# Moving a never-taken branch of a fused RWKV and mixture-of-experts kernel ahead of the last expert's products

## The chip, the cores and the metric

The kernel runs on one core of a Trainium2 chip. The metric is the device time of one execution in microseconds (us). Three runs of the kernel before took 984.41, 988.21 and 988.93 us; the median is 988.21 us. One execution was also profiled, instruction by instruction.

TensorE is written PE here (its weight loads PEld), VectorE DVE, ScalarE ACT, GpSimd POOL and SyncE SP. A "q" behind a name (PEldq, POOLq) marks what the engine's sequencer does by itself: branches, semaphore waits, drains. L1002 is line 1002 of the kernel's file.

## The reference, cut to what matters

```python
x = x + rwkv(layernorm(x), ...)        # time mixing: 4 sequences of 1024 tokens, 256 channels
x = x + moe(layernorm(x), ...)         # 8 experts, 2 for each token

def moe(hidden):                       # 256 -> 896 -> 256
    weights = softmax(hidden @ gate_w.T)
    # each token goes to its two best experts; in one sequence an expert
    # takes at most capacity = 320 tokens, in order of the tokens
    h1, h3 = dispatch @ w1, dispatch @ w3
    return combine(silu(h1) * h3 @ w2)
```

With four sequences an expert gets between 0 and 1280 rows; the mean is 4096 x 2 / 8 = 1024. How many it gets is known only at run time.

## The kernel before

**Layout of the work.** The time mixing goes block by block (256 tokens) through the four sequences. After each group of tokens the router writes the rows, by scatters on POOL, into a buffer in device memory (`disp`). There each expert owns 11 tiles of 128 rows. The tiles are worked on in five stages, `TILES = (0, 1, 3, 5, 9, 11)` (L42): stage 0 is tile 0 of every expert, stage 3 is tiles 5 to 8, and stage 4 is tiles 9 and 10, the rarely filled ones. The constant `B` is 4 and `E` is 8, so stage 4 is written `B` in the code.

**One expert's stage** is the generator `expert(e, s)` (L839). It issues four loads on SP: the weights w1, w3, w2 (`load_w`, L834, memory tag "w", five buffers) and the rows `xe` (L852). PE transposes the rows (L873), DVE copies them to `xeT` (L877). Then `hidden` (L887) makes seven pairs of products with w1 and w3 (L904), ACT takes silu (`sl`, L909), DVE multiplies (`act`, L893, eight buffers, of which one stage of an expert holds seven at a time). `results` (L919) multiplies by w2 (L925), DVE scales by the router's weight (`ye`, L929), and POOL adds each tile of 128 rows to the output by an indirect DMA (L932). Each such DMA carries explicit dependencies on the previous expert's output DMAs (`last["adds"]`), since two experts add to the same token's row.

**The order.** `experts_in_turn` (L979) takes a list of (expert, stage) jobs. For each job it yields the seven pairs of products, then starts the next job's loads and transposes ("ahead"), then finishes the results. Stages 0 to 2 are interleaved with the time mixing; stage 3 of the eight experts runs after it, one expert after the other, and PE has nothing else to do there. In stage 3 only three of the four tiles are sure to be needed (`SURE = 3`). The fourth stands inside `tc.If(flags(e) > 0)` (L1002). In this data the branch is taken for three experts and skipped for five, expert 6 and expert 7 among these. Stage 4 of all eight experts stands in one last branch, `tc.If(flags(E) > 0)` (L1150), at the very end. It is never taken in this data.

**What a branch is.** On each of the five engines it is a compare-and-branch, the taken body, and a short body for "not taken". The short body waits until the engine itself has done all that it had been given, then raises the engine's semaphores by as much as the taken body would have. On POOL it also waits for the outstanding indirect DMAs and raises their semaphores with one instruction (INC_SWDGE_SEM); on SP it waits for outstanding loads where the body holds loads. No engine waits for another there. The compiler's scheduler places instructions around a branch per engine; it may put instructions that come earlier in the program behind a branch, and later ones in front of it. In the trace of before, DVE's last `ye` and POOL's last output DMA of an expert come behind that expert's branch.

After the last branch each engine drains, SP waits for every DMA and engine semaphore, and two barriers over all engines end the program (line L1188 in the profile).

Of the kernel before, what the change touches and what calls it, by code (L numbers as in the profile page):

```python
# [9 lines left out]
F32 = mybir.dt.float32  # L10
# [7 lines left out]
P = 128  # L18
B, T, C = 4, 1024, 256
NT = B * T  # L20
H, N = 16, 16
CC = C // P
HC = H // CC
TB = 256
# [3 lines left out]
RT = RB // P  # L28
RPS = T // RB
ST = T // P  # L30
E, FF = 8, 896
FC = FF // P
# [13 lines left out]
W = C + 1 + E  # L46
# [19 lines left out]
def rwkv_then_moe_kernel(  # L66
# [12 lines left out]
    nc = tc.nc  # L79

    const = ctx.enter_context(tc.tile_pool(name="const", bufs=1))
    keep = ctx.enter_context(tc.tile_pool(name="keep", bufs=1))
    a1 = ctx.enter_context(tc.tile_pool(name="a1", bufs=1))
    a2 = ctx.enter_context(tc.tile_pool(name="a2", bufs=2))
    sm = ctx.enter_context(tc.tile_pool(name="sm", bufs=1))
    fp = ctx.enter_context(tc.tile_pool(name="ffn", bufs=2))
# [4 lines left out]
    def bank(tag, name):  # L91
        return ps.tile(
            [P, 512], F32, tag=tag, name=name, bufs={"m": 4, "y": 1, "f": 3}[tag])
# [42 lines left out]
    def maa(m, cc):  # L136
# [10 lines left out]
        out=tri, in_=ones, pattern=[[1, P]], compare_op=ALU.is_ge, fill=0.0,  # L147
# [5 lines left out]
        out=bd, in_=ones[:, :HC], pattern=[[-N, HC]], compare_op=ALU.is_ge, fill=0.0,  # L153
# [3 lines left out]
        out=bd, in_=bd, pattern=[[N, HC]], compare_op=ALU.is_ge, fill=0.0,  # L157
# [36 lines left out]
    wmat = const.tile([P, H, P], F32, tag="wmat", name="wmat")  # L194
# [639 lines left out]
    def load_w(ap, rows_, nm):  # L834
        t = fp.tile([P, rows_, FF * CC // rows_], F32, tag="w", name=nm, bufs=5)
        nc.sync.dma_start(out=t, in_=ap.rearrange("(k p) n -> p k n", p=P))
        return t

    def expert(e, s):  # L839

        nm = f"{e}_{s}"
        n = TILES[s + 1] - TILES[s]
        r0 = e * SLOTS + TILES[s] * P
        after = tc.issue_after(cleared) if s == 0 and e < 2 else nullcontext()
        with after:
            w1e = load_w(w1[e], CC, f"w1_{nm}")
            w3e = load_w(w3[e], CC, f"w3_{nm}")
            w2e = load_w(w2[e], FC, f"w2_{nm}")  # L850
        xe = fp.tile([P, n, W], F32, tag="xe", name=f"xe{nm}")
        load = nc.sync.dma_start(  # L852
            out=xe, in_=disp[r0:r0 + n * P, :].rearrange("(s p) c -> p s c", p=P)).ins
        for g in range(len(SEGMENTS)):
# [8 lines left out]
                    reason="rows of this expert")  # L863
        if s < B:
            tc.add_to_no_dep_group(f"load{s}", load)
        xeT = fp.tile([P, CC, n * P], F32, tag="xeT", name=f"xeT{nm}")
        pts = [bank("f", f"pe{nm}")] * CC
        if n > 2:
            pts[1] = bank("f", f"pe{nm}_1")
        for cc in range(CC):  # L870
# [11 lines left out]

        def tag(t0):

            return "m" if t0 else "f"

        def hidden(t0, t1):  # L887
            lo, w = t0 * P, (t1 - t0) * P
            acts = []

            def product(sl, p3, f):
                act = fp.tile([P, w], F32, tag="act", name=f"act{nm}_{t0}_{f}", bufs=8)
                nc.vector.tensor_tensor(act, sl, p3[:, :w], ALU.mult)  # L893
                acts.append(act)

            for f in range(FC):
                p1 = bank(tag(t0), f"p1_{nm}_{t0}_{f}")
                if 2 * w <= 512:
                    p3 = p1[:, w:]
                else:  # L900
                    p3 = bank(tag(t0), f"p3_{nm}_{t0}_{f}")
                for pp, wt in ((p1, w1e), (p3, w3e)):
                    for cc in range(CC):
                        nc.tensor.matmul(  # L904
                            pp[:, :w], wt[:, cc, f * P:(f + 1) * P], xeT[:, cc, lo:lo + w],
                            start=cc == 0, stop=cc == CC - 1,
                        )
                sl = fp.tile([P, w], F32, tag="sl", name=f"sl{nm}_{t0}_{f}")
                nc.scalar.activation(sl, p1[:, :w], AF.Silu)  # L909
                if f:  # L910
                    product(*held)
                held = sl, p3, f
                yield 2 * CC * w
            product(*held)
            return acts
# [3 lines left out]
        def results(t0, t1, acts):  # L919
            ye = fp.tile([P, t1 - t0, C], F32, tag="ye", name=f"ye{nm}_{t0}", bufs=3)  # L920
            for t in range(t0, t1):
                i = t - t0
                po = bank(tag(t0), f"pw2_{nm}_{t}")
                for f in range(FC):
                    nc.tensor.matmul(  # L925
# [43 lines left out]
    def due(s):  # L969
        g = AFTER[s]  # L970
        return g in clock.routed and clock.step >= clock.routed[g] + LAGS[s]

    def flags(e):

        if "flags" not in last:
            _, last["flags"] = nc.values_load_multi_w_load_instructions(last["over"][0:1, :])
        return last["flags"][e]

    def experts_in_turn(jobs):  # L979

        ahead = None
        for i, (e, s) in enumerate(jobs):
            while ahead is None:
                if s >= B or due(s):
                    ahead = expert(e, s)
                    clock.turn = min(s, B - 1)
                    yield next(ahead)
                    yield None
                else:
                    yield None  # L990
            now, ahead = ahead, None
            for _ in range(FC):
                yield next(now)
            if i + 1 < len(jobs) and (jobs[i + 1][1] >= B or due(jobs[i + 1][1])):
                ahead = expert(*jobs[i + 1])
                clock.turn = jobs[i + 1][1]
                yield next(ahead)
            for cols in now:
                if cols is not None:
                    yield cols  # L1000
                    continue
                with tc.If(flags(e) > 0):  # L1002
                    for _ in now:
                        pass

    def routed(b, r):
# [12 lines left out]
    def fronts(n):  # L1019
        if n >= NBLK:  # L1020
            return iter(()), None
        b, blk = divmod(n, BPS)
        o = Block()
        return front(b, blk, o), o

    work = experts_in_turn([(e, b) for b in range(B) for e in range(E)])


# [7 lines left out]
    f, cur = fronts(0)  # L1036
# [27 lines left out]
    with tc.issue_after(cleared):  # L1064
        r0 = (B - 1) * T
        nc.sync.dma_start(
            out=out[r0:r0 + EK * P, :].rearrange("(k p) c -> p k c", p=P),
            in_=empty[0][:, :, :C])
# [13 lines left out]
    with tc.manual_schedule(engines={ENG.PE}):  # L1082
        for n in range(NBLK):
# [11 lines left out]
            c = [chunk(b, blk, t, cur) for t in range(TPB)]  # L1095
            new = back(b, blk, cur)
            for i, stage in enumerate((
# [23 lines left out]
                while credit > 0 or drain:  # L1121
                    drain = False
                    cols = next(work, None)
# [23 lines left out]
        nc.vector.tensor_copy(last["over"], over)  # L1147
        for _ in work:
            clock.step += 1
    with tc.If(flags(E) > 0):  # L1150
        for _ in experts_in_turn([(e, B) for e in range(E)]):
            pass


# [37 lines left out]
```

## Time and profile before

| | us |
|---|---|
| median of three runs | 988.21 |
| the profiled execution | 987.89 |
| its span, first to last instruction | 986.2 |
| PE busy | 943.5 (96%) |
| expert 6, stage 3: products with w1, w3 on PE | 920.26 to 938.48 |
| expert 6: results on PE | 939.20 to 948.53 |
| expert 7, stage 3: products with w1, w3 on PE | 948.83 to 967.13 |
| expert 7: results on PE, the last matmul's end | 966.96 to 976.19 |
| last output DMA on POOL | 976.99 to 978.54 |
| end of the span | 986.17 |

Times inside the profile count from the first instruction. The difference of 1.7 us between the profiled execution's time and its span lies outside what the profile shows. The page gives an engine's busy time, groups of instructions by line with the idle time ahead of them and what ended it, and the granted clock of TensorE (PEclk, 1.00 is full speed). Sequencer rows are not busy time; they are read from the view of a single line.

### The profile page before, as it was taken

What the parts mean: (1) busy time and instruction counts of PE and PEld (TensorE: products, weight loads), DVE (VectorE), ACT (ScalarE), POOL (GpSimd) and SP (SyncE); (2) the same over time, 40 slices, a digit from 0 to 9 for tenths busy, and PEclk for the clock granted to TensorE, in tenths of its full rate; (3) what the DMA queues carried; (4) which work ended last, traced back from release to release, by engine and by line L of the source; (5) the groups of instructions that cost most, each with busy time, mean ns of one, the idle gap of its engine ahead of it and who ended that gap; (6) DMA issues with size and microseconds to landing.
All of it is one profiled execution on the core that took longest, in us unless ns stands there. A gap on an engine that the chain in (4) does not pass through costs nothing. (4 is left out here: it accounts for less than half of the span.)

```text
span 986.2 us, 17107 instructions
## 1 busy us (share of the span) xinstructions
PE 943.5 (96%) x6758; PEld 748.7 (76%) x6758; DVE 454.5 (46%) x1317; ACT 318.2 (32%) x797; POOL 249.1 (25%) x267
## 2 busy tenths in 40 slices
PE   7899889999999799999999999999999999999995
PEld 6667677888788588887888788888866866867764
DVE  7888857666676544435453434422222222222221
ACT  6636545544653532243414123211110111111110
POOL 6321512422117312111163211361111111211111
PEclk9999999999999999999999999999999999999998
DMA  4995132534435544342465544586545235433421
GB/s 154 264 288 187 50 99 98 199 119 132 156 122 206 162 124 126 104 145 73 122 183 173 157 134 156 158 272 182 156 144 151 44 113 150 134 81 103 145 54 19
DMA packets 92073, 139.06 MB, mean 141 GB/s; under 512 B 5456, under 2 KB 73552, under 8 KB 91984
## 3 DMA queue, kind: packets, MB, share of 16 engines
q1 hardware_dynamic: 79120, 120.36, 37.6%
q0 software_dynamic: 12720, 17.47, 9.2%
q8 instruction: 58, 0.95, 0.4%
q14 instruction: 31, 0.25, 0.1%
q10 hardware_dynamic: 144, 0.02, 0.0%
HBM read 103.45 MB, written 34.39 MB: 140 GB/s over the span
## 5 line engine op out<-in xcount | busy, mean ns | idle before, releaser
L904 PE MATMUL p<-xeT,w 128*128 128x256 f32 (+2 forms) x1960 | 430.6, 374 | 3.6 <-DVE act L893 1.8
L904 PEld LDWEIGHTS p<-xeT,w 128*128 128x128 f32 x1960 | 326.3, 191 | 93.8 <-issue 8.6
L893 DVE TENSOR_TENSOR act<-sl,p 128x256 f32<-128x256 f32 (+2 forms) x245 | 99.2, 407 | 294.3 <-ACT sl L909 178.2
L909 ACT ACTIVATE sl<-p 128x256 f32<-128x256 f32 (+2 forms) x245 | 91.0, 374 | 438.8 <-PE p L904 436.2
L925 PE MATMUL pw<-w,act 128*128 128x256 f32 x938 | 210.5, 380 | 1.2 <-DVE act L893 1.2
L932 POOL DMA_INDIRECT y_out<-ye,xe x67 | 105.4, 1573 | 405.0 <-DVE ye L929 346.9
L925 PEld LDWEIGHTS pw<-w,act 128*128 128x128 f32 x938 | 175.3, 190 | 25.7 <-DVE act L893 2.3
L929 DVE TENSOR_SCALAR ye<-pw,xe 128x256 f32<-128x256 f32 x67 | 32.2, 483 | 126.0 <-PE pw L925 125.9
L499 DVE TENSOR_TENSOR aw<-pa,wmat 128x512 f32<-128x512 f32 x128 | 79.3, 682 | 8.0 <-PE pa L491 8.0
L416 PE MATMUL pc<-xm,wa 128*128 128x256 f32 x256 | 68.6, 417 | 10.1 <-DVE xm L406 5.9
L804 POOL DMA_INDIRECT disp<-hs,is x64 | 63.9, 998 | 26.8 <-issue 15.5
L416 PEld LDWEIGHTS pc<-xm,wa 128*128 128x128 f32 x256 | 51.2, 207 | 22.2 <-DVE xm L406 6.2
L340 ACT ACTIVATE aside<-x 128x256 f32<-128x256 f32 x60 | 24.9, 416 | 82.2 <-DVE x L604 81.4
L406 DVE SCALAR_TENSOR_TENSOR xm<-xx,ch,xT 128x256 f32<-128x256 f32 x96 | 42.8, 477 | 12.5 <-POOL xx L400 7.7
L491 PE MATMUL pa<-rT,kT 32*128 32x256 f32 x512 | 40.2, 401 | 0.7 <-DVE upd L539 0.7
L520 PE MATMUL y<-aw,vpad 128*32 128x128 f32 x1024 | 40.5, 278 | 0.0
L443 POOL TENSOR_TENSOR xm_g<-xx,ch 128x512 f32<-128x512 f32 x16 | 17.7, 1109 | 84.6 <-PE pc L416 75.4
L550 POOL TENSOR_TENSOR state<-state,upd 128x64 f32<-128x64 f32 x24 | 8.2, 341 | 120.4 <-DVE upd L539 109.2
L599 PE MATMUL po<-wa,zT 128*128 128x256 f32 x128 | 30.8, 383 | 6.1 <-DVE zT L591 4.5
L520 PEld LDWEIGHTS y<-aw,vpad 128*32 128x32 f32 x1024 | 24.4, 109 | 12.2 <-issue 11.4
L491 PEld LDWEIGHTS pa<-rT,kT 32*128 32x128 f32 x512 | 25.2, 184 | 8.5 <-issue 3.5
L453 PE MATMUL pt<-wa,xm 128*128 128x256 f32 x128 | 30.8, 383 | 0.9 <-DVE rbT L436 0.9
(183 smaller groups left out, 826.1 us busy)
## 6 DMA issues: line engine op xcount, KB each, us to landing
w<-w_in SPq DMA_DIRECT2D x96, 896.0 KB, 6.0
disp<-empty SPq DMA_DIRECT2D x8, 795.0 KB, 14.3
disp<-empty SPq DMA_DIRECT2D x16, 265.0 KB, 7.2
xe<-disp SPq DMA_DIRECT2D x16, 265.0 KB, 2.7
xe<-disp SPq DMA_DIRECT2D x8, 530.0 KB, 3.7
y_out<-x SPq DMA_DIRECT2D x8, 512.0 KB, 3.0
x<-x_in SPq DMA_DIRECT2D x7, 512.0 KB, 6.5
wa<-w_attn_in SPq DMA_DIRECT2D x5, 256.0 KB, 4.3
```

Source lines behind the costliest of these rows:

```text
L406: last["xm"] = nc.vector.scalar_tensor_tensor(xm[:, cc, :], xx[:, cc, :], maa(m, cc), xT[:, cc, 1:TB + 1], ALU.mult, ALU.add,).ins
L416: nc.tensor.matmul(pp[:, m * TB:(m + 1) * TB], wa[w][:, cc, m * P:(m + 1) * P], xm[:, cc, :], start=cc == 0, stop=cc == CC - 1,)
L491: nc.tensor.matmul(pa[g][:, cc * TB:(cc + 1) * TB], o.kT[rows32, cc, cols], o.rT[rows32, cc, :, cols], start=True, stop=True, tile_positio ...
L499: nc.vector.tensor_tensor(w.rearrange("p q i -> p (q i)"), pa[g], wmat[:, 4 * g:4 * g + 4, :].rearrange("p q i -> p (q i)"), ALU.mult,)
L520: nc.tensor.matmul(y[32 * g:32 * g + 32, :], o.vp[:, t, cc * 4 + g, q * 32:(q + 1) * 32], aw[g][:, cc * 2 + q, :], start=state is None and ...
L804: ins = nc.gpsimd.indirect_dma_start(out=disp[:, :], out_offset=bass.IndirectOffsetOnAxis(ap=idx_s[g][:, c, t:t + 1], axis=0), in_=last["h ...
L893: nc.vector.tensor_tensor(act, sl, p3[:, :w], ALU.mult)
L904: nc.tensor.matmul(pp[:, :w], wt[:, cc, f * P:(f + 1) * P], xeT[:, cc, lo:lo + w], start=cc == 0, stop=cc == CC - 1,)
L909: nc.scalar.activation(sl, p1[:, :w], AF.Silu)
L925: nc.tensor.matmul(po[:, :C], acts[f][:, i * P:(i + 1) * P], w2e[:, f, :], start=f == 0, stop=f == FC - 1,)
L929: nc.vector.tensor_scalar_mul(ye[:, i, :], po[:, :C], xe[:, t, C + 1 + e:C + 2 + e])
L932: ins = nc.gpsimd.indirect_dma_start(out=out[:, :], out_offset=bass.IndirectOffsetOnAxis(ap=xe.bitcast(I32)[:, t, C:C + 1], axis=0), in_=y ...
```

## The change

The branch with stage 4 leaves the end of the program and moves into `experts_in_turn`, behind the flag branch of the last expert but one (expert 6, stage 3). At that place expert 7's stage 3 has been started ("ahead": its loads are issued or queued, its rows transposed), and its products with w1, w3, w2 follow behind the moved branch. The program now ends with the flag branch of expert 7.

So that the branch does not take the memory in which expert 7's operands stand, its tiles lie elsewhere: w1 and w3 in halves in the buffers of `x` (tag "x", four buffers, each half loaded by a DMA of its own), w2 in the buffer of `wmat`, the rows in tag "hs", the transposed rows in tag "xx", and the PSUM banks under tag "m" in place of "f". The time mixing and the router have left these; the last access to any of them in the trace of before is at 656.9 us. The tags `act`, `sl` and `ye` are still shared. No buffer changes its size. For stages 0 to 3 the code is as before.

```diff
+    class Halves:
+        def __init__(self, ap, nm):
+            self.parts = []
+            for cc in range(CC):
+                t = keep.tile([P, RT, C], F32, tag="x", name=f"w{nm}_{cc}", bufs=4)
+                t = t.rearrange("p t c -> p (t c)")[:, :FF]
+                nc.sync.dma_start(out=t, in_=ap[cc * P:(cc + 1) * P, :])
+                self.parts.append(t)
...
     def expert(e, s):
...
+        if s < B:
...
+        else:
+            w1e, w3e = (Halves(ap[e], f"{i}_{nm}") for i, ap in ((1, w1), (3, w3)))
+            w2e = const.tile([P, H, P], F32, tag="wmat", name=f"w2_{nm}").rearrange(
+                "p h i -> p (h i)")[:, :FC * C].rearrange("p (f c) -> p f c", f=FC)
+            nc.sync.dma_start(out=w2e, in_=w2[e].rearrange("(k p) n -> p k n", p=P))
+            xe = a2.tile([P, RT, W], F32, tag="hs", name=f"xe{nm}")[:, :n, :]
...
-        pts = [bank("f", f"pe{nm}")] * CC
+        pts = [bank("f" if s < B else "m", f"pe{nm}")] * CC
...
-            return "m" if t0 else "f"
+            return "m" if t0 or s >= B else "f"
...
                 with tc.If(flags(e) > 0):
                     for _ in now:
                         pass
+            if jobs[i + 1:] == [(E - 1, B - 1)]:
+                with tc.If(flags(E) > 0):
+                    for _ in experts_in_turn([(k, B) for k in range(E)]):
+                        pass
...
         for _ in work:
             clock.step += 1
-    with tc.If(flags(E) > 0):
-        for _ in experts_in_turn([(e, B) for e in range(E)]):
-            pass
```

More of the change, by code (lines that the diff above doesn't have):

```diff
@@ L837, in load_w, with __getitem__ @@
         return t
+    class Halves:
[6 more added lines that the diff above has]
+                self.parts.append(t)
+        def __getitem__(self, at):
+            rows_, cc, cols = at
+            return self.parts[cc][rows_, cols]
     def expert(e, s):
@@ L846, in expert @@
         after = tc.issue_after(cleared) if s == 0 and e < 2 else nullcontext()
[L847 to L851, printed above, removed]
+        if s < B:
+            with after:
+                w1e = load_w(w1[e], CC, f"w1_{nm}")
+                w3e = load_w(w3[e], CC, f"w3_{nm}")
+                w2e = load_w(w2[e], FC, f"w2_{nm}")
+            xe = fp.tile([P, n, W], F32, tag="xe", name=f"xe{nm}")
+        else:
[4 more added lines that the diff above has]
+            xe = a2.tile([P, RT, W], F32, tag="hs", name=f"xe{nm}")[:, :n, :]
         load = nc.sync.dma_start(
@@ L865, in expert @@
             tc.add_to_no_dep_group(f"load{s}", load)
-        xeT = fp.tile([P, CC, n * P], F32, tag="xeT", name=f"xeT{nm}")
-        pts = [bank("f", f"pe{nm}")] * CC
+        if s < B:
+            xeT = fp.tile([P, CC, n * P], F32, tag="xeT", name=f"xeT{nm}")
+        else:
+            xeT = a1.tile([P, CC, TB], F32, tag="xx", name=f"xeT{nm}")
+        pts = [bank("f" if s < B else "m", f"pe{nm}")] * CC
         if n > 2:
```

## The prediction

> **What bounds the kernel now.** I read the page's busy shares first, then the timeline around expert 6 and the end, then the lines of the two branches one by one, then the granted clock in windows.
>
> ```profile
> PE 943.5 (96%) x6758; PEld 748.7 (76%) x6758; DVE 454.5 (46%) x1317; ACT 318.2 (32%) x797; POOL 249.1 (25%) x267
> ```
>
> PE is busy for 96% of the span. What matters is whether PE idles, and what lies behind its last matmul. The timeline:
>
> ```profile
> 939.20 9.33 PE L925 MATMUL pw<-w,act 128*128 128x256 f32 x42
> 948.83 18.30 PE L904 MATMUL p<-xeT,w 128*128 128x384 f32 x56 [0.30 <-PEq L1002]
> ...
> 966.96 9.23 PE L925 MATMUL pw<-w,act 128*128 128x256 f32 x42
> 976.99 1.55 POOL L932 DMA_INDIRECT y_out<-ye,xe  x1 [1.47 <-DVEq L1150]
> ```
>
> The second row is expert 7's first products: a skipped flag branch (L1002) costs PE 0.30 us. The last matmul ends at 976.19, the span at 986.17: 9.98 us of tail. The view of line L1150, the branch that moves:
>
> ```profile
> L1150 PEldq COMPARE_BRANCH  x1: 3650/3650/3650, 976.4 to 976.4; - x1
> L1150 POOLq COMPARE_BRANCH  x1: 45/45/45, 976.8 to 976.8; - x1
> L1150 DVEq EVENT_SEMAPHORE  x1: 21/21/21, 976.8 to 976.8; - x1
> L1150 PEldq EVENT_SEMAPHORE  x1: 51/51/51, 980.1 to 980.1; - x1
> L1150 POOLq INC_SWDGE_SEM  x1: 1012/1012/1012, 980.8 to 980.8; - x1
> ```
>
> and PE's row for the eight flag branches (three of them taken, which gives 11 records), with the end (L1188):
>
> ```profile
> L1002 PEldq COMPARE_BRANCH  x11: 70/180/356, 747.5 to 972.2; - x11
> ```
>
> ```profile
> L1188 POOLq DRAIN  x3: 46/107/3458, 981.9 to 985.9; - x3
> ```
>
> (Columns: count, shortest/median/longest in ns, first and last start in us.) On PE the moved branch takes 3.65 us, a flag branch at most 0.36. It jumps over eight experts: 28 + 14 products of two passes and 4 transposes, each pass a weight load and a matmul, are 176 instructions for an expert, 1408 in all; a flag branch jumps over 140. The instruction queue moved 0.95 MB in 58 packets, and one packet of 16 KB started at 977.69, inside the 3.65 us: PE was waiting for its code. Now this costs nothing: PE has no work left, and POOL's last output DMA lands only at about 980.75, when its wait for it ends.
>
> **The change, part by part.**
>
> *What PE pays.* Behind the end of expert 6's results PE's queue would hold: flag branch, moved branch, expert 7's products. At the end of before, semaphore to semaphore of the two branches is 976.24 to 980.09, so 3.85 us, all of it PE idle if nothing stands between them. Something may: the moved branch must come behind expert 6's last output DMA (its first output DMA depends on that one), and that DMA is issued at 949.33, when PE has already started on expert 7. Matmuls of expert 7 that the scheduler puts ahead of the branch run while the code is fetched. The trace shows the rates: at 944.50 PE's sequencer reached the flag branch, with 4.03 us of matmuls (18 pairs) still to run, so it runs ahead; the 84 instructions of those results were handed out from 939.2 to 944.5, 0.063 us each, 0.13 for a pair, while a pair with 384 columns runs for 18.30 / 56 = 0.327. Each pair ahead thus hides about 0.2 us. The bounds: no pair ahead, 3.85; and 16 pairs, 3.85 - 16 x 0.2 = 0.65. More is not possible by much, since expert 7 may hold one of the eight `act` buffers at most when the branch needs seven. I take the four pairs that run between 948.83 and the issue of expert 6's last output DMA (0.5 us, rounded up to whole products of one pair of operands): 3.85 - 4 x 0.2 = **+3.0**.
>
> *What the clock takes.* PE then idles for about 3.0 to 3.3 us. The windows view (us; PE, PEld, DVE, ACT, POOL busy; PEclk; DMA) shows what followed such a gap:
>
> ```profile
> 120.70:124.10 3.40, 1.24 (x11) 0.80 (x12) 2.92 (x15) 3.32 (x12) 0.73 (x3) 1.00 0.47 155
> 124.10:127.50 3.40, 3.40 (x9) 2.58 (x10) 1.62 (x3) 2.34 (x7) 0.00 (x0) 0.50 0.57 149
> ...
> 328.90:332.30 3.40, 0.28 (x2) 0.28 (x3) 2.10 (x4) 1.58 (x5) 2.22 (x3) 1.00 0.54 161
> 332.30:335.70 3.40, 3.40 (x12) 2.77 (x11) 3.37 (x12) 0.00 (x0) 1.71 (x2) 0.50 0.74 227
> ```
>
> At 328.9 PE had idled 3.19 us for a load; in the next 3.4 us the clock was 0.50 and eight matmuls took 607 ns each against 379 elsewhere. A window with 1.24 us of work was followed by half a clock too. Half a clock for 3.4 us of work loses 1.7. The windows' edges are fixed (the two drops are 61 x 3.41 us apart), so it depends on where the gap falls: it must put over some 2.1 us into one window. A gap of 3.0 does so in (0.41 + 2 x 0.9) / 3.41, two of three cases. I take 1.0 (bounds 0 and 1.7).
>
> [...]
>
> *What the tail gives back.* Without the branch, POOL needs no wait for the last landing and no INC_SWDGE_SEM (1.01) ahead of its drain. It can drain from 978.54, the end of its last output DMA's instruction, in place of 981.88. With its 3.46 us it is through at 982.0 in place of 985.34 (times as in before, PE's delay left out): **-3.34**. Next late is then SP: its waits go on from the landing at 980.75 and, by their present pace (twelve waits and the drain from 981.80 to 983.1, so 1.2 us for what follows this landing), end at about 982.0 too, so a shorter drain would give no more. At worst the drain can only start to count from the landing: 980.75 + 3.46 = 984.2, a gain of 1.1. I take 3.3, since the drain has no semaphore to wait for.
>
> *What costs nothing, and its cover.* ACT's and DVE's part of the branch is 45 + 17 and 56 + 21 ns; DVE's next instruction for expert 7 came at 951.75, three us behind its last `ye`. SP: w2 of expert 7 was issued at 948.65; behind the moved branch's eight waits (0.5 us; every earlier load has landed) it would be issued some 1 us later, lands within 6.6 and is needed at 966.96. POOL: the branch waits for expert 6's last output DMA (until about 954.4) and takes 1.0; POOL's next work came at 970.95. Should one of these jumps wait for code as PE's did, 3.65 us fit into each of these covers but DVE's, and DVE's work is itself delayed by PE's gap. The new tiles: their loads and copies lie in the branch that isn't taken; the extra DMAs (six for an expert in place of four) are not issued. Stages 0 to 3 keep their buffers, and what `x`, `hs`, `xx` and `wmat` held was last used at 656.9 us.
>
> **Sum:** +3.0 + 1.0 - 3.3 = +0.7 us. From the profiled execution's 987.89 that is **988.6**; the three runs' median, 988.21, lies 0.3 above the profiled execution, which is far inside their own spread of 4.5 us.
>
> **How it could go otherwise.**
>
> *The fetch is hidden.* The scheduler waits for expert 6's last output DMA to land (3.8 to 5.1 us behind its issue) before it places the branch, so that 12 to 16 pairs run first. PE then pays about 0.7 and no clock is lost: 0.7 - 3.3 = -2.6, so **985.3**, and 984.8 if PE pays as little as 0.2. For it: the dependency is on the data, not on the issue. Against: the output DMAs of one expert's branch may be ordered by issue alone.
>
> *The tail is not given back.* The drain starts to count at the landing (gain 1.1), and PE pays in full, with the clock: 3.85 + 1.4 - 1.1 = +4.2, so **992.1**. For it: that drain is 3.46 us long, and the profile names nothing that it waits for.
>
> *Slower: a second fetch.* PE's jump lands near the end of a block of code. At the end of before the next block's packet started only at 980.79, 3.1 us behind the first one's and 0.7 behind the end of the branch; like the first (977.69, usable at 980.03) it would be usable 2.3 later, 3.0 us behind PE's restart. So if fewer than 9 pairs plus what the queue takes ahead, some 20 to 30 of a block's 235 instructions (0.95 MB for PE's 13,516 are 70 bytes each), are left where the jump lands, PE stops again, by up to 3 us, and the clock stays at one half for two windows, 3.4 lost in place of 1.0: 0.7 + 3.0 + 2.4 = +6.1, so **994.0**. That place is decided by the code's length alone: about 1 in 9.
>
> *It doesn't do what it says.* The scheduler could put the branch behind expert 7's products after all; the `act` buffers exclude it, since all seven would be held.
>
> **How the numbers follow.** A measurement of this kernel can tell about 0.5% from no change, 4.9 us. The forecast (986.8 to 990.5 by its own bounds) has 0.50; the hidden fetch 0.22; the tail not given back 0.14; the second fetch 0.11; no effect 0.03. The range takes in all but the second fetch: from 984.8 (hidden fetch at its best) to 992.4 (full price, full loss of clock, 1.1 from the tail: +4.45). Faster by over 0.5% means below 983.0, which only the hidden fetch with a still shorter tail reaches: 0.06. Slower means above 992.8: the second fetch and a third of the tail's case, 0.16. Within: 0.78.
>
> **What would show it.** PE's row of the moved branch again near 3.65 us, at about 949 to 953; a gap in PE's timeline of 3.0 to 4.2 us there, by its length the number of matmuls ahead; PEclk 0.50 in the window behind it; no INC_SWDGE_SEM behind POOL's last output DMA, and a tail of 6.6 us in place of 9.98. It is wrong if PE's branch is short in its new place (then the time falls by 3 us), if the tail keeps its 9.98, or if the gap exceeds 5 us.

## The result, and the profile after

The changed kernel's median is 990.73 us over 11 runs, against 987.5 us for the kernel before in its 11. One run of the kernel before, at 4534 us, was disturbed; without it the median of the other ten is 986.9, and the ratio leaves it out. The ratio is 1.0034, with a 95% interval of 1.002 to 1.0048: about 3.3 us slower, clear of noise, though inside 0.5%. The profiled execution is the slowest of the 11 (993.48 us, span 991.7), so the terms read from its trace may be larger than the usual ones.

The view of the moved branch's line, after (columns: count, shortest/median/longest in ns, first and last start in us):

```profile
L1032 POOLq EVENT_SEMAPHORE  x4: 17/43/6601, 950.1 to 956.9; - x4
L1032 DVEq COMPARE_BRANCH  x1: 56/56/56, 949.1 to 949.1; - x1
L1032 PEldq COMPARE_BRANCH  x1: 5085/5085/5085, 949.3 to 949.3; - x1
L1032 PEldq EVENT_SEMAPHORE  x1: 51/51/51, 954.4 to 954.4; - x1
L1032 POOLq INC_SWDGE_SEM  x1: 935/935/935, 957.0 to 957.0; - x1
```

DVE passes in 56 ns. POOL waits 6.6 us for the output DMAs and holds up nobody, since its next work is at 979.65. PE waits 5.09 us for its code, in place of 3.65. PE's timeline (start, length, count; in brackets the idle time ahead and what ended it):

```profile
939.73 9.33 PE L951 MATMUL pw<-w,act 128*128 128x256 f32 x42
954.65 21.18 PE L930 MATMUL p<-xeT,w 128*128 128x384 f32 x56 [5.59 <-PEq L1032]
975.67 9.23 PE L951 MATMUL pw<-w,act 128*128 128x256 f32 x42
```

The second row starts 5.59 us behind the end of the first, where it was 0.30, and lasts 21.18 us, where it was 18.30. The windows view says why (us; busy us of PE, PEld, DVE, ACT, POOL; PEclk; DMA share; GB/s):

```profile
949.00:952.50 3.50, 0.06 (x1) 0.00 (x0) 0.48 (x1) 0.00 (x0) 1.55 (x1) 1.00 0.76 147
952.50:956.00 3.50, 1.35 (x2) 0.84 (x3) 0.00 (x0) 0.00 (x0) 0.00 (x0) 0.66 0.73 203
956.00:959.50 3.50, 3.50 (x7) 1.92 (x6) 0.00 (x0) 0.49 (x1) 0.00 (x0) 0.50 0.01 1
959.50:963.00 3.50, 3.50 (x10) 1.96 (x10) 0.55 (x1) 0.49 (x1) 0.00 (x0) 0.86 0.00 0
963.00:966.50 3.50, 3.50 (x12) 2.08 (x11) 1.11 (x2) 0.49 (x1) 0.00 (x0) 1.00 0.02 5
```

The granted clock fell to one half, for 6.83 us in all (953.6 to 960.5 in the trace's clock records): 7 matmuls in a window that holds 12 at full clock. The first two rows also show the DMA engines 76% and 73% busy. Part of that is expert 7's w2, issued at 949.18, 0.07 us ahead of PE's branch:

```profile
949.18 0.37 SPq L836 DMA_DIRECT2D w<-w_in  x1
```

The tail:

```profile
L1214 POOLq DRAIN  x3: 46/113/5359, 985.5 to 991.4; - x3
L1214 SPq DRAIN  x3: 7/7/7, 990.0 to 991.1; - x3
```

From the last matmul's end (984.90) to the end of the span (991.66) it is 6.76 us, where it was 9.98.

The sum for this execution: the gap +5.29 (5.59 - 0.30), the half clock +2.88 (21.18 - 18.30), the tail -3.22: +4.95. The spans differ by 5.5; the other 0.5 was there before the change begins to act (the end of expert 6's results is at 949.06, in place of 948.53). Over all runs the difference is 3.3.

### The profile page after: what moved, and what is told of

It reads as the page before. It is cut to its first block, busy times and chain, and to the rows that moved or that the text cites. A ratio compares the mean times of both kernels' runs of the same rounds, so it can differ in the third digit from the quotient of the medians.

```text
span 991.7 us, 17110 instructions
## 1 busy us (share of the span) xinstructions
PE 946.3 (95%) x6758; PEld 750.0 (76%) x6758; DVE 454.7 (46%) x1317; ACT 318.5 (32%) x797; POOL 249.2 (25%) x267
```

## The experiments

**The theory.** In its new place PE's wait for code lies on the path that sets the end. It is longer there (5.09 us, against 3.65 at the end of before), because w2's load shares the DMA engines with the fetch. The idle time then halves the clock (PEclk 0.50 from 956.0 to 959.5). The tail gives back 3.2 us, and the new memory costs nothing. **The rivals:** the new memory brings waits of its own; the branch costs by its semaphore work or its place, not by the length of the code that it skips; the tail gives nothing back.

Times here are compared as ratios to runs of the kernel before from the same occasion (median 992.91 us for experiments 1 to 4, 986.80 for 5 to 8). One execution of each kernel was profiled.

**1. The memory alone.** Stage 4's new tiles, its branch at the end as before.

```diff
-            if jobs[i + 1:] == [(E - 1, B - 1)]:
-                with tc.If(flags(E) > 0):
...
+    with tc.If(flags(E) > 0):
+        for _ in experts_in_turn([(e, B) for e in range(E)]):
+            pass
```

> The new tiles for stage 4, but its branch at the end as before. Theory (the time comes from PE's wait for code in the new place, and from the half clock behind it; the new memory costs nothing since its tiles lie in the branch not taken): ratio to before 1.000 within 0.1%, PE's row of the branch 3.65 us at the end, a tail of 10.0 us behind the last matmul. Rival (the tiles in the buffers of x, wmat, hs and xx bring new waits or another order of loads): 1.002 to 1.0035, with a gap on PE somewhere before the last expert.

Measured: ratio 0.9994 (0.998 to 1.0008). Its profile has the small gap between the experts, and the fetch at the end:

```profile
954.16 18.30 PE L930 MATMUL p<-xeT,w 128*128 128x384 f32 x56 [0.30 <-PEq L1028]
```

```profile
L1176 PEldq COMPARE_BRANCH  x1: 3690/3690/3690, 981.7 to 981.7; - x1
```

The tail is 10.07 us. The memory is not the cause, and the rival of new waits falls.

**2. No branch.** Stage 4 is left out.

```diff
-            if jobs[i + 1:] == [(E - 1, B - 1)]:
-                with tc.If(flags(E) > 0):
-                    for _ in experts_in_turn([(k, B) for k in range(E)]):
-                        pass
```

> As changed, but the branch with stage 4 is left out altogether (stage 4 is not computed; in this data it is never taken). Theory: no gap on PE between experts 6 and 7 but 0.3 us, full clock there, and the short tail of 6.8 us: 3.2 us less than before, ratio 0.9967 (0.996 to 0.9975). Rival (the tail gives nothing back by itself, other work fills it): 0.999 to 1.001.

Measured: ratio 0.9974 (0.996 to 0.9988), 2.6 us less than before; the tail is 6.68 us, and the gap and the products are as in the kernel before:

```profile
956.62 18.30 PE L930 MATMUL p<-xeT,w 128*128 128x384 f32 x56 [0.30 <-PEq L1028]
```

So the branch at the end did cost some 3 us. It did so by what stands on POOL and not by PE's fetch: in the trace of before PE is through with the branch at 980.09, POOL's semaphore instruction ends at 981.85 and its drain at 985.34.

**3. The fetch without the load beside it.** Expert 7 multiplies by expert 6's w2, so that its own isn't loaded.

```diff
-                w2e = load_w(w2[e], FC, f"w2_{nm}")
+                if (e, s) == (E - 1, B - 1):
+                    w2e = last["w2"]
+                else:
+                    w2e = load_w(w2[e], FC, f"w2_{nm}")
+                last["w2"] = w2e
```

> As changed, but expert 7's stage 3 uses expert 6's w2, so that the 0.9 MB load of its own w2, which is issued as PE's branch begins, is left out (expert 7's rows come out wrong). Theory (the fetch took 5.1 us in place of 3.65 because its 16 KB packet, 2.39 us in place of 1.03, shares the DMA engines with that load): PE's branch 3.6 to 3.9 us, its packet 1.0 to 1.2, gap about 4.2; 1.4 us less than the changed kernel, ratio to before 1.0015 to 1.0025. Rival (the fetch in the middle is longer by itself, since its place in the code differs): PE's branch 5.0 again, ratio 1.003 to 1.004.

Measured: ratio 1.0019 (1.0006 to 1.0031). The branch, the windows and the timeline of PE in its profile:

```profile
L1036 PEldq COMPARE_BRANCH  x1: 3515/3515/3515, 955.1 to 955.1; - x1
```

```profile
955.00:958.50 3.50, 0.00 (x0) 0.00 (x0) 0.41 (x1) 0.00 (x0) 1.55 (x1) 1.00 0.50 63
958.50:962.00 3.50, 3.02 (x5) 1.84 (x6) 0.00 (x0) 0.04 (x1) 0.00 (x0) 0.55 0.13 21
```

```profile
958.98 19.92 PE L934 MATMUL p<-xeT,w 128*128 128x384 f32 x56 [4.09 <-PEq L1036]
```

The wait is 3.52 us. The DMA engines are still half busy (0.50), at 63 GB/s in place of 147 and 203. The 16 KB packet took 1.07 us by the DMA records, against 2.39 in the changed kernel and 1.03 at the end of before. So 1.4 to 1.6 us of the 5.09 come from the load beside it. The clock still fell, for one window of 3.41 us in place of two: 19.92 - 18.30 = 1.62 us. The two kernels' ratios are each against before and their intervals overlap; it is the profiles that separate the theory from its rival.

**4. One expert in the body.** Seven experts' stage 4 is left out.

```diff
-                    for _ in experts_in_turn([(k, B) for k in range(E)]):
+                    for _ in experts_in_turn([(k, B) for k in range(1)]):
```

> As changed, but the moved branch holds stage 4 of one expert in place of eight (the other seven are left out; never taken in this data): it jumps over about 180 of PE's instructions in place of 1400. Theory (length of the code): PE's branch 0.1 to 0.4 us, gap on PE 0.5 to 0.8, clock stays 1.00, tail 6.8: ratio 0.997 to 0.9975. Rival (the semaphore work of a second branch, or its waits for output DMAs, holds PE up, whatever its length): gap 4 us and more, ratio 1.001 to 1.0035.

Measured: ratio 0.9968 (0.995 to 0.9987). The branch at the same place, with the same semaphore work:

```profile
L1032 PEldq COMPARE_BRANCH  x1: 217/217/217, 951.5 to 951.5; - x1
```

```profile
952.12 18.30 PE L930 MATMUL p<-xeT,w 128*128 128x384 f32 x56 [0.83 <-PEq L1032]
```

The gap is 0.83, the clock stays full. The place and the semaphores cost 0.5 us (0.83 - 0.30); all else is the length of the code. No 16 KB packet started inside this branch. The tail was 7.18 here, a little longer than the 6.7 to 6.9 of the other kernels without the branch at the end.

**5 and 6. Two and four experts** (one run each, 984.69 and 987.52 us; the other experts' stage 4 is left out). The edit is that of experiment 4 with `range(2)` and `range(4)`.

> As changed, with two experts in the branch's body (352 of PE's instructions, some 25 KB at 70 bytes, one and a half blocks of 16 KB). [...] Rival (the wait grows with the bytes skipped): about a quarter of 5.1, 1.0 to 1.6 us.

```profile
L1032 PEldq COMPARE_BRANCH  x1: 457/457/457, 948.0 to 948.0; - x1
```

> As changed, with four experts in the body (704 instructions, some 49 KB, three blocks). Theory (one block is fetched, however far the jump goes): PE's branch 3.6 to 5.3 us as with eight experts, 16 KB in one packet inside it. Rival (the wait grows with the bytes skipped): about half, 2.0 to 2.8 us.

```profile
L1032 PEldq COMPARE_BRANCH  x1: 4365/4365/4365, 945.0 to 945.0; - x1
```

```profile
949.69 2.90 PE L930 MATMUL p<-xeT,w 128*128 128x384 f32 x4 [4.87 <-PEq L1032]
952.84 16.93 PE L930 MATMUL p<-xeT,w 128*128 128x384 f32 x52 [0.26 <-issue]
```

So 0.22, 0.46, 4.37 and 5.09 us for some 176, 352, 704 and 1408 instructions: a step between two and four experts. The difference between the first two is no slope that these runs can tell, since skipped flag branches over 140 instructions took 0.23 to 0.36 in the traces of before and of the changed kernel. With two experts no 16 KB packet started inside the branch; with four one did and took 2.16 us, beside w2's load, which fits a wait nearer to 5.09 than to 3.65. The rival of a wait that grows with the bytes skipped falls.

With four experts PE stopped a second time, for 0.26 us after four matmuls. The next block's packet ran from 950.16 to 951.43, and PE's weight loads went on at 952.84, 1.41 us later; behind the first packets of these branches 1.1 to 1.5 us passed before PE went on. That fits the second fetch which the prediction named as a rival, most of it hidden since the matmuls ran at half clock; no experiment was made on it.

**7. Behind seven pairs of products.** The branch goes once more, to between expert 7's products and its results; stage 4's `act` lie in the buffers of `aw`, since expert 7 holds seven of the eight `act` buffers there.

```diff
+                if s < B:
...
+                else:
+                    if f % 2 == 0:
+                        pair.append(a2.tile([P, 4, P], F32, tag="aw", name=f"act{nm}_{f}", bufs=4).rearrange("p q i -> p (q i)"))
+                    act = pair[-1][:, f % 2 * w:(f % 2 + 1) * w]
...
-            for _ in range(FC):
+            for f in range(FC):
                 yield next(now)
+                if (e, s, f) == (E - 1, B - 1, FC - 1):
+                    with tc.If(flags(E) > 0):
+                        for _ in experts_in_turn([(k, B) for k in range(E)]):
+                            pass
...
-            if jobs[i + 1:] == [(E - 1, B - 1)]:
-                with tc.If(flags(E) > 0):
-                    for _ in experts_in_turn([(k, B) for k in range(E)]):
```

> The branch moved once more: behind expert 7's seven pairs of products and ahead of its results, with stage 4's act tiles in the buffers of aw (nothing else may hold seven more). Theory (the fetch costs only what PE's queue does not cover): PE's sequencer comes to the branch some 18 weight-load-and-matmul pairs, about 5.9 us, ahead of PE and fetches while they run; gap on PE under 0.6 us, clock stays 1.00, expert 7's products 18.3 us, tail 6.8: ratio 0.9965 to 0.9975, as with no branch at all. Rival (any second branch in the middle empties PE's queue and makes it wait for code, wherever it stands): gap 3.6 us and more, ratio 1.001 to 1.0035.

Measured: ratio 0.9969 (0.9955 to 0.9984), 3.1 us less than before. This version beats both kernels and still holds stage 4, though no run here takes that branch. The branch's line and PE's timeline:

```profile
L1026 PEldq COMPARE_BRANCH  x1: 3289/3289/3289, 963.5 to 963.5; - x1
L1026 PEldq EVENT_SEMAPHORE  x1: 51/51/51, 967.0 to 967.0; - x1
```

```profile
948.52 18.30 PE L935 MATMUL p<-xeT,w 128*128 128x384 f32 x56 [0.30 <-PEq L1037]
967.22 9.30 PE L956 MATMUL pw<-w,act 128*128 128x256 f32 x42 [0.40 <-PEq L1026]
```

The same fetch takes 3.29 us, from 963.53 to 966.82, just as the products end at 966.82; expert 7's w2 had landed at 954.33. PE's gap is 0.40 us. The sequencer came to the branch only 3.3 us ahead of PE, not 5.9 as expected; the fetch just fits.

**8. Behind two pairs of products,** otherwise as in experiment 7 (`f` is 1).

> The same with the branch behind the first two of expert 7's seven pairs of products: 16 weight-load-and-matmul pairs ahead, 5.2 us of work handed out in about 2. Theory: PE's branch 3.65 to 5.1 us, of which 3.2 are covered; gap on PE 0.7 to 2.3 us, the clock at one half in some executions only; ratio 0.998 to 1.000. Rival (no cover): gap 4 us and more, 1.002 to 1.0035.

Measured: ratio 0.9991 (0.9973 to 1.0008), PE's branch 4.98 us, and

```profile
L1026 PEldq COMPARE_BRANCH  x1: 4976/4976/4976, 948.0 to 948.0; - x1
```

```profile
945.81 5.40 PE L935 MATMUL p<-xeT,w 128*128 128x384 f32 x16 [0.30 <-PEq L1037]
953.12 14.83 PE L935 MATMUL p<-xeT,w 128*128 128x384 f32 x40 [1.91 <-PEq L1026]
```

Of the wait 3.24 us (947.97 to 951.21) ran under the 16 pairs ahead; a gap of 1.91 was left. It halved the clock for one window: the two rows take 20.23 us together in place of 18.30. The wait was partly covered, and the ratio lies between those of the changed kernel and of experiment 7. The wait was long although the 16 KB packet took only 1.03 us: it started 2.66 us behind the branch's start, where it was 1.0 to 1.3 us in the other kernels with a fetch. Expert 7's w2 was being loaded at that time (945.63 to 951.80). That the load held the packet up ahead of its start is likely, but no run here shows it.

The same products in experiment 2 without any branch, and in 7 with it, take 18.30 us at full clock, and the two ratios agree: with 3.3 us of work queued ahead, the branch costs nothing that the ratios can tell; PE's timeline has its gap of 0.40 us.

## Why the prediction was right or wrong, point by point

The direction of the forecast (slightly slower, within 0.5%) and the range held. The forecast of +0.7 us was short by 2.6 us, and two of its terms were wrong. By its own sign ("if the gap exceeds 5 us") the account was wrong on PE's side, since the gap was 5.59. That the range held was partly luck: the prediction's full price (3.85), full loss of clock (1.7) and the tail at 3.3 make +2.25, less than the measured +3.3, and the rest of the room came from a tail case that did not occur. The forecast's own band, 986.8 to 990.5, missed 990.73 by a little; it does not follow from the bounds given with it, which end at 987.89 + 2.25 = 990.1.

- **What PE pays** was put at +3.0. The step that failed is "I take the four pairs that run between 948.83 and the issue of expert 6's last output DMA". No pair stood ahead: the scheduler placed the branch directly behind expert 6's last output DMA and before any product of expert 7, though on PE these had started 0.5 us earlier in the kernel before. Here the time at which records start on different engines did not tell the order in which the scheduler placed them. With no pair ahead the bound given was 3.85. That was exceeded too, at 5.29, because the price of the fetch was read at the end of the program, where no load of weights ran beside it (DMA share 0.39 to 0.40 in before, 0.73 to 0.76 here). The prediction counted w2's load only for its own landing and not as a competitor of the fetch, and it expected the load some 1 us later, behind the moved branch on SP; SP issued it at 949.18, ahead of its branch at 949.60. Without that load the gap is 4.09 (experiment 3), 3.79 more than 0.30: the bound itself was right.
- **What the clock takes** was put at 1.0, with a bound of 1.7. It took 2.88 in the profiled execution, 1.62 in experiment 3 and 1.93 in experiment 8. The bound had counted one window; here the gap of 5.59 us reached 1.0 us into a second, and two windows ran at half clock (6.83 us in the clock records), where gaps of 4.09 and 4.87 us (experiments 3 and 6) cost one; one lasts 3.41 us there. Gaps of 0.83 and 0.96 us (experiments 4 and 5) cost none, a gap of 1.91 us did, all of it in one window; the prediction had asked for some 2.1. A window of before with 1.70 us of work in 3.50, from 130.9 us, so 1.80 us idle, was followed by full clock (PEclk 1.00 from 134.4 to 137.9 us). What set the 1.80 us apart from the 1.91, no run here shows.
- **What the tail gives back** was put at 3.3 and is 3.22. The reason was partly wrong: POOL's drain did not become free at once, but starts earlier and lasts longer (5.36 us), and ends 3.58 us behind the end of POOL's last output DMA. It is still the last, 0.7 us behind SP.
- **What costs nothing** cost nothing: the memory (experiment 1), and the parts of ACT, DVE, SP and POOL. w2 landed 7.0 us after its issue, at 956.2; PE's first use of it is at 975.67.
- **The rivals.** The hidden fetch did not happen by itself; experiment 7 brings it about, and its price, 985.3 for a kernel of 987.9 (-2.6 us), is near what it measured (-3.1). The tail that isn't given back is refuted by experiment 2. The second fetch did not hold PE up in the changed kernel: the next block's packet started 0.76 us after the branch ended, and no second gap followed. In experiment 6 one of 0.26 us did, so the rival was a real one.

What stays open: how far the spread of the changed kernel's runs (985.32 to 993.48) comes from where the gap falls in the clock's windows and how far from the fetch. Only one execution of each kernel was profiled. Open is also how a load holds the fetch up: the packet itself took 2.16 and 2.39 us in two kernels, and in experiment 8 it started late instead.

## What to carry to other kernels

The branch was paid here by PE, which skips some 1408 instructions in it (a wait of 5.09 us, where DVE passed in 56 ns), and the price is a fetch that the engine's queue can hide: put such a branch where that engine has as much work queued as the fetch lasts (3.3 us in experiment 7), not right behind another branch that empties the queue. At the very end the same fetch (3.65 us in before) was free, for nothing followed it; there the branch was paid elsewhere, by the waits of POOL ahead of its drain (2.6 us by experiment 2). Before moving a wait, ask what else uses the DMA engines in the new place (they were 76% busy here), and whether the gap is long enough to halve TensorE's clock: here that was a third to a half of what PE lost (2.88 of 8.17 us in the changed kernel, 1.93 of 3.84 in experiment 8).

## What the runs showed of the hardware

- A skipped body of some 176 and 352 PE instructions cost the branch 0.22 and 0.46 us, one of 1408 a wait of 3.3 to 3.7 us without a load of weights at the same time and 5.0 to 5.1 us beside a load of 0.9 MB, one of 704 a wait of 4.4 us beside such a load. Where between 352 and 704 instructions the step lies, and what sets it, no run here shows.
- The code's 16 KB packet took 1.03 and 1.07 us without the load, 2.16 and 2.39 us beside it. In experiment 8 it took 1.03 us beside the load, but started 2.66 us behind the branch's start in place of 1.0 to 1.3.
- POOL's final drain ended 3.5 to 3.6 us after the last thing POOL had to do with its own DMAs, whether that was an output DMA (3.58 after, in the changed kernel) or the semaphore instruction (3.49 after, in the kernel before).
